# Late images' first quartic by moved tiles, and a rearranged end, in a matrix-root and spectral-convolution kernel

## The chip, the cores and the metric

The kernel runs on one core of a Trainium2 chip. A core has a matrix engine (PE, with its weight loads PEld), a vector engine (DVE), a scalar engine (ACT), GpSimd (POOL) and a sync engine (SP) that only issues DMAs; ACT's queue can issue DMAs too. Each engine works off its own queue in order. The metric is device microseconds of one execution, taken as the median of the runs.

## The reference, cut to what matters

Input x has 32 images of 32 channels, each a 128x128 matrix in 32-bit floats. Two layers follow each other:

```python
def _L0_conv_ref(A):            # matrix square root by Newton-Schulz, 5 steps
    Y = A2 / normA[:, None, None]; Z = I
    for _ in range(5):
        T = 0.5 * (3.0 * I - Z @ Y)
        Y = Y @ T
        Z = T @ Z
    return Y * sqrt(normA)

x = x + _L0_conv_ref(_gn(x))            # _gn: group norm, 16 groups of 2 channels
x = x + _L1_conv_ref(_gn(x), weights1, weights2)
# _L1: 2-d Fourier transform of each channel, the lowest 32 columns and
# 32 + 32 rows of it mixed over channels by weights that differ per mode,
# inverse transform, real part
```

The result is x after both layers.

## The kernel before, in words

**Newton groups.** The root is computed on groups of four channels, 8 groups per image and 256 in all. A group is a generator, `newton`; a `yield` ends a call. The five Newton steps are folded into two quartic polynomials and a last quadratic, so a group makes ten sets of four 128x128 products. Every product needs one operand transposed, and there are two ways to get it. *Near* groups (image 0 and images 19 to 31; `FIRST` is 19) transpose on PE: in `near_quartic` the vector `v` is transposed there, once in each quartic, and `newton` transposes `m` once between them. *Far* groups (images 1 to 18) transpose blocks of 32x32 on DVE (`turned`) and let DMAs put the blocks in place: `across` moves from tile to tile in four DMAs, `away` and `back` go through device memory. The far quartic works with `by_rows`, a view of the moved tile.

**Order.** The order on each engine is the order in which Python issues the instructions. The loop at the end of the kernel works in rounds: it visits nine lanes, calls each lane's group once, and gives steps to side queues in between: `norms` (staging: scaled copies `m` and `mb` of a group, on POOL and ACT), `preps` (statistics of images two ahead, from `xs` tiles), `posts` (`settle`: the store to `mid`, the folds, the statistics of the second layer; then `forward`), `specs` (`spectrum`), `prods` (products with the weights) and `backs` (`inverse`). A far group is started every 26/9 rounds, a near one every 25/5, with at most `LESS` (5) near groups under way. `stage` and `fetch` run ahead: when a group starts, the next is staged and the inputs `b` and `xt` of the third next are fetched.

**The convolution.** It is done in sets of images: `GROUPS` is 20, 7, 3, 2. When a set's last spectrum is there, its products follow (`wide_products` for 20, `small_products` for 7 and 3, `last_products` for the last two), through the tensors `xs`, `od` and `or` in device memory, and then an `inverse` per image: `place` reorders the products into `ob`, PE makes `gt` (tab,ob) and then, in two halves e, four banks `py` (gt,tab), each with a cosine part of 65 columns and a sine part of 63. ACT copies the sine part to `d`, DVE adds the cosine part to both halves of `y` (loaded from `mid`), and `unfold` subtracts and adds `d` on POOL (or DVE for half of them in the tail). `store` writes `y` out, by SP, or by ACT's queue in the tail, when no lane works any more.

**Room.** Tiles come from reserves per name (`rooms`: so many of a pool that lasts, and so many of a pool `early` that is closed when 158 groups are settled). `weights` fetches the weights for `last_products` into tiles that the last groups no longer need.

Of the kernel before, what the change touches and what calls it, by code (L numbers as in the profile page):

```python
# [36 lines left out]
P = 128  # L37
# [56 lines left out]
def conv_preact_kernel(  # L94
# [51 lines left out]

    stp = ctx.enter_context(tc.tile_pool(name="stp", bufs=4))
    up = ctx.enter_context(tc.tile_pool(name="up", bufs=1))
# [73 lines left out]
    def prep(bs, made):  # L222
# [7 lines left out]

        ahead = 3 if first_b else 8

# [74 lines left out]

    rooms = dict(b=(4, 6), xt=(10, 5), x=(3, 2), r=(4, 0), v=(3, 2), w=(3, 2), q=(4, 2))
    rooms.update(my=(4, 3), mb=(2, 4), t=(3, 2), y4=(2, 2), turn=(0, 4))
    turns = dict.fromkeys(rooms, 0)  # L310
# [46 lines left out]
    def is_far(b):  # L357
        return 0 < b < FIRST
# [7 lines left out]
    def fetch(b, g):  # L366
        queue = nc.sync if is_far(b) else nc.scalar
        xt, t = four("xt", has_more(b, g)), four("b", has_more(b, g))
        kept(queue.dma_start(out=t, in_=x[b, :, 4 * g : 4 * g + 4, :]))
        kept(queue.dma_start(out=xt, in_=xt_in[b, :, 4 * g : 4 * g + 4, :]))  # L370
        raw[b, g] = xt, t
# [3 lines left out]
    def staged(b, g, nm, sc, off, sn):  # L375
# [10 lines left out]
        for j in range(4):  # L386
            c = 4 * g + j
            if j < 2 or not is_far(b):
                kept(
# [17 lines left out]
    def near_quartic(m, mb, more):  # L407


        v = plus(m, -QA * MS, products(mb, m), "v", more)  # L410
        yield
        r = four("r", more)
        nc.gpsimd.tensor_tensor(r, mb, eye, ALU.add)
# [24 lines left out]

    def by_rows(t):
        return blocks(t).rearrange("p a c j -> p c a j")  # L440

    def across(t, more):
# [10 lines left out]
        return w  # L453

    def far_quartic(m, mb, v, f, later, more):

        ps = products(m, mb)
        if later:
            held = away(turned(ps, more))
        else:  # L460
            w = across(turned(ps, more), more)
        if later:
            yield
        nc.vector.scalar_tensor_tensor(v, ps, 1 / (9 * MS), v, ALU.mult, ALU.add)
# [13 lines left out]

    def newton(g, sn, xt, m, mb, v, far, more):


        qf, et, eye_t = (QS, EYE_Q, eye_q) if far else (QF, EYE, eye)
        if far:
            q = yield from far_quartic(m, mb, v, 1.0, False, more)
        else:
            q = yield from near_quartic(m, mb, more)
# [24 lines left out]
        else:  # L511
# [3 lines left out]
            yield from rest  # L515
            q = yield from near_quartic(m, mb, more)
            both = [bank().rearrange("p (j k) x -> p j k x", k=2) for _ in range(2)]
            for j in range(4):
# [224 lines left out]
    def small_products(i):  # L743
# [38 lines left out]
        for k2 in range(len(xks)):  # L782
            load_spectra(k2)
        done = None
        for kk in range(KK):
# [36 lines left out]
    def last_products(i):  # L822


        for e in range(2):
            load_input(B - GROUPS[i], e)
        for kk in range(KK):
            if kk % 4 == 0:
                yield
                om = page(f"om{i}_{kk}").rearrange("p (f s o) -> p s f o", f=4, s=8)  # L830
            if kk % 2 == 0:
# [21 lines left out]
            if kk % 4 == 3:  # L853
                for f in range(4):
# [6 lines left out]
                    )  # L861
        warm(9)
        yield

    def weights():


        kinds = [("b", 2)] * 3 + [("x", 2), ("b", 4), ("x", 4), ("x", 10)]
        kinds += [("my", 11)] * 2 + [("r", 12)] * 3 + [("mb", 15)] * 2 + [("v", 15)] * 2
        kinds += [("w", 16)] * 2 + [("my", 16), ("r", 17), ("v", 18)] + [("q", 19)] * 3  # L870
        first = B * C // 4 - 10
# [66 lines left out]
    holding = []  # L938

    def unfold():  # L940

        while sums:
            b, o, y, d = sums.pop(0)
            engine = nc.vector if tail and o % 16 else nc.gpsimd
            for half, op in enumerate((ALU.subtract, ALU.add)):
                yh = y[:, :, 64 * half : 64 * half + 64]
                engine.tensor_tensor(yh, yh, d, op)
            stores.append((b, o, y))

# [20 lines left out]
    def inverse(b):  # L970
# [161 lines left out]
    while todo or any(lanes) or posts or specs or prods or backs:  # L1132
# [3 lines left out]
        for i in range(LANES):  # L1136
# [3 lines left out]
            under_way = [is_far(lane[0]) for lane in lanes if lane]  # L1140
            room = far or under_way.count(False) + 0.6 * under_way.count(True) < LESS
            if lanes[i] is None and todo and room and rounds >= due:
# [4 lines left out]
                xt = ready[0][0]  # L1147
                lanes[i] = (b, g, xt, newton(g, made[b][3], *ready.pop(0), far, has_more(b, g)))
                if stages:
# [91 lines left out]
```

## Time and profile before

| | |
|---|---|
| median of 3 runs | 2969.88 us (2962.28 to 2977.81) |
| the profiled execution's own time | 2972.83 us |
| its span, first to last instruction | 2971.0 us |
| PE, PEld busy | 96%, 90% |
| DVE, ACT, POOL busy | 76%, 52%, 67% |
| DMA | 674.22 MB, mean 227 GB/s |
| PE ident,v (transpositions of v) | 896 instructions, mean 277 ns |
| PE w,v and others (products) | 279 ns mean, two instructions per 128x128 product |
| first group of image 19 starts | about 1498 us |
| last group starts | about 2851 us |
| first instruction of the last set's products | 2917 us |

The tile names in the profile are the program's (`ps<-ident,v` is a PE instruction that writes a bank `ps` and reads `ident` and `v`). All instructions pass through one helper, so their line is always L88, and names tell them apart. `SPq` and `ACTq` are DMA issues. The mean of a PE instruction is from its start to its modelled end, and neighbours overlap; the distance of starts is what it holds the engine for.

### The profile page before, as it was taken

Reading aid. Unit: us, or ns where it says so; the run is one execution under the profiler, and the core shown is the slowest. Engines: PE = TensorE matmul, PEld = TensorE weight load, DVE = VectorE, ACT = ScalarE, POOL = GpSimd, SP = SyncE. Lnnn points to the kernel's source line nnn. Section 1 sums busy time; section 2 is a strip of 40 time slices with the busy share of each in tenths; the row PEclk is TensorE's granted clock in tenths of the full one; section 3 lists DMA queues with packets and bytes.
Section 4 is the critical chain, followed back from the end, with each engine's and each line's share of the span. In section 5 each row is a group of like instructions: output and inputs, shape, how many; then the busy total and the mean of one; then the engine's idle time right before and its main releaser. Section 6 shows DMA issues by size and latency. Waiting matters only on the chain.

```text
span 2971.0 us, 74313 instructions
## 1 busy us (share of the span) xinstructions
PE 2847.8 (96%) x27688; PEld 2666.9 (90%) x27688; DVE 2270.9 (76%) x4407; ACT 1544.7 (52%) x3899; POOL 1986.9 (67%) x2308
## 2 busy tenths in 40 slices
PE   7999999999999999999999999999999999999995
PEld 7899999998999999999999889888888999888983
DVE  7779788888788888888886645886787766777565
ACT  3555555555555555555544445555555544655552
POOL 4677777776767777777665534877778764678453
PEclk9999999999999999999999999999999999999997
DMA  5687878787787878787843566767767747766577
GB/s 174 185 250 244 242 242 251 240 257 231 233 252 217 275 228 263 236 253 239 270 145 98 164 209 210 269 217 271 269 228 268 273 127 222 218 223 225 180 221 260
DMA packets 553078, 674.22 MB, mean 227 GB/s; under 512 B 99344, under 2 KB 333840, under 8 KB 552720
## 3 DMA queue, kind: packets, MB, share of 16 engines
q1 hardware_dynamic: 480576, 536.53, 56.9%
q10 hardware_dynamic: 72144, 132.94, 14.3%
q8 instruction: 222, 3.64, 0.5%
q14 instruction: 136, 1.11, 0.1%
HBM read 402.42 MB, written 229.11 MB: 213 GB/s over the span
## 4 chain that ended last, share of the span: by engine, by line
PE 66%; POOL 11%; DMA 9%; issue 7%; DVE 5%; ACT 1%; SPq 1%; ACTq 0%; DVEq 0%; POOLq 0%
PE ps L88 66%; POOL yt L88 3%; POOL r L88 3%; POOL x L88 2%; DMA w<-turn 2%; POOL fold L88 2%; DMA yt<-mid 1%; DMA b<-in_x 1%; DMA xt<-in_xt 1%; SPq L88 1%; DVE turn L88 1%; DMA xs<-in_xs 1%; DVE yt L88 1%; DMA mid<-xt 1%; DMA out<-yt 1%
## 5 line engine op out<-in xcount | busy, mean ns | idle before, releaser
L88 ACT ACTIVATE my<-ps 128x512 f32<-128x512 f32 x512 | 305.3, 600 | 563.6 <-PE ps L88 443.7
L88 POOL TENSOR_TENSOR fold<-xt 128x256 f32<-128x256 f32 x512 | 363.5, 732 | 285.9 <-DVE xt L88 257.2
L88 ACT ACTIVATE b<-b,a_off,a_sc 128x128 f32<-128x128 f32 x1024 | 469.8, 493 | 97.1 <-issue 15.9
L88 PE MATMUL ps<-my,q 128*128 128x128 f32 (+1 forms) x2944 | 474.4, 309 | 5.7 <-ACT my L88 3.8
L88 PEld LDWEIGHTS ps<-my,q 128*128 128x128 f32 x2944 | 412.9, 192 | 33.0 <-ACT my L88 4.6
L88 POOL TENSOR_TENSOR v<-eye_v,b 128x512 f32<-128x512 f32 x144 | 183.6, 1275 | 382.9 <-ACT b L88 344.6
L88 POOL TENSOR_TENSOR yt<-yt,d 128x512 f32<-128x512 f32 x244 | 306.8, 1281 | 187.4 <-ACT d L88 155.3
L88 PE MATMUL ps<-w,v 128*128 128x128 f32 x2944 | 399.9, 279 | 13.0 <-DVE w L88 10.6
L88 PEld LDWEIGHTS ps<-w,v 128*128 128x128 f32 x2944 | 363.5, 194 | 22.3 <-issue 7.6
L88 DVE STREAM_TRANSPOSE turn<-ps 128x512 f32<-128x512 f32 x432 | 299.7, 702 | 62.2 <-PE ps L88 57.1
L88 ACT ACTIVATE t<-ps 128x256 f32<-128x256 f32 (+1 forms) x368 | 171.0, 467 | 333.3 <-PE ps L88 316.7
L88 POOL TENSOR_SCALAR x<-xt,a_nm,a_sc 128x128 f32<-128x128 f32 x736 | 321.2, 450 | 15.8 <-DVE a_sc L88 15.5
L88 ACT ACTIVATE y<-ps,a_t_s 128x128 f32<-128x128 f32 x1024 | 291.4, 371 | 45.2 <-PE ps L88 45.1
L88 PE MATMUL ps<-q,t 128*128 128x128 f32 x2048 | 273.8, 277 | 0.8 <-DVE v L88 0.8
L88 DVE SCALAR_TENSOR_TENSOR w<-ps,r 128x512 f32<-128x512 f32 x224 | 153.1, 684 | 139.3 <-POOL r L88 71.2
L88 PEld LDWEIGHTS ps<-q,t 128*128 128x128 f32 x2048 | 249.6, 192 | 3.3 <-issue 1.2
L88 DVE BATCH_NORM_STATS2 a_st<-xs 128x6 f32<-128x256 f32 x504 | 185.9, 410 | 64.9 <-DMA xs<-in_xs 64.6
L88 DVE SCALAR_TENSOR_TENSOR q<-ps,eye 128x512 f32<-128x512 f32 x224 | 153.3, 684 | 97.6 <-PE ps L88 94.8
L88 DVE TENSOR_TENSOR xt<-ps,xt 128x512 f32<-128x512 f32 x256 | 174.7, 683 | 40.7 <-PE ps L88 35.2
L88 POOL TENSOR_TENSOR r<-mb,eye 128x512 f32<-128x512 f32 x112 | 142.9, 1276 | 91.8 <-ACT mb L88 91.8
L88 DVE TENSOR_TENSOR yt<-ps,yt 128x512 f32<-128x512 f32 x256 | 163.3, 681 | 39.9 <-PE ps L88 34.4
L88 POOL TENSOR_TENSOR my<-eye_q,my 128x512 f32<-128x512 f32 x144 | 183.8, 1277 | 7.5 <-PE ps L88 7.5
(147 smaller groups left out, 6284.9 us busy)
## 6 DMA issues: line engine op xcount, KB each, us to landing
turn<-turn SPq DMA_DIRECT2D x288, 256.0 KB
mid<-xt SPq DMA_DIRECT2D x256, 256.0 KB
yt<-mid SPq DMA_DIRECT2D x128, 512.0 KB
xs<-in_xs ACTq DMA_DIRECT2D x252, 256.0 KB
out<-yt SPq DMA_DIRECT2D x115, 512.0 KB
b<-in_x SPq DMA_DIRECT2D x144, 256.0 KB
xt<-in_xt SPq DMA_DIRECT2D x144, 256.0 KB
w<-turn SPq DMA_DIRECT2D x576, 64.0 KB
```

Source lines behind the costliest of these rows:

```text
L88: return self.tc.keep_in_program_order(issue(*args, **kw))
```

## The change

1. Groups of images 19 to 31 use a new `late_quartic` as their first quartic: DVE's block transposition and `across` in place of the PE transposition of `v`. The second quartic stays `near_quartic`, in which `r` is now issued a call earlier. These groups' fetches go by SP, and half of the staging of `m` goes from POOL to ACT, as for far groups. Up to six near groups may be under way when no far one is.
2. The reserves are divided anew, and `xs` tiles are six instead of four, loaded five ahead instead of three.
3. Output stores wait until two rounds after their `unfold`, and are looked for in each round.
4. In the last group's calls from the 22nd on, and while products are pending in the tail, no inverse step is issued. `last_products` uses `fold` tiles for the first three of its outputs, and nine warming products at its end go; six are issued in the tail where an inverse loads.
5. For images 30 and 31, the upper and the lower half of an output row are summed in the bank `py` by PE, with a table and its negative, and DVE adds the bank to `y` once: no `d`, no `unfold`.

```diff
-    stp = ctx.enter_context(tc.tile_pool(name="stp", bufs=4))
+    stp = ctx.enter_context(tc.tile_pool(name="stp", bufs=6))
...
-        ahead = 3 if first_b else 8
+        ahead = 5 if first_b else 8
...
-    rooms = dict(b=(4, 6), xt=(10, 5), x=(3, 2), r=(4, 0), v=(3, 2), w=(3, 2), q=(4, 2))
-    rooms.update(my=(4, 3), mb=(2, 4), t=(3, 2), y4=(2, 2), turn=(0, 4))
+    rooms = dict(b=(5, 5), xt=(10, 4), x=(3, 2), r=(3, 0), v=(3, 2), w=(3, 2), q=(3, 3))
+    rooms.update(my=(3, 4), mb=(2, 4), t=(2, 3), y4=(2, 2), turn=(2, 2))
...
-        queue = nc.sync if is_far(b) else nc.scalar
+        queue = nc.sync if b else nc.scalar
...
-            if j < 2 or not is_far(b):
+            if j < 2 or not b:
...
     def near_quartic(m, mb, more):
-        v = plus(m, -QA * MS, products(mb, m), "v", more)
-        yield
         r = four("r", more)
         nc.gpsimd.tensor_tensor(r, mb, eye, ALU.add)
+        v = plus(m, -QA * MS, products(mb, m), "v", more)
+        yield
         yield
         w = plus(transposed(v), 1.0, r, "w", more)
...
+    def late_quartic(m, mb, more):
+        v = minus(eye_v, m, four("v", more))
+        ps = products(mb, m)
+        t = turned(ps, more)
+        yield
+        nc.vector.scalar_tensor_tensor(v, ps, 1 / (9 * MS), v, ALU.mult, ALU.add)
+        w = across(t, more)
+        yield
+        minus(eye_q, mb, mb)
+        yield from rest
+        yield from rest
+        q = plus(products(v, by_rows(w)), 9 / (39 * MS**2), mb, "q", more)
+        yield from rest
+        return q
...
-    def newton(g, sn, xt, m, mb, v, far, more):
-        qf, et, eye_t = (QS, EYE_Q, eye_q) if far else (QF, EYE, eye)
+    def newton(g, sn, xt, m, mb, v, far, late, more):
+        qf, et, eye_t = (QS, EYE_Q, eye_q) if far or late else (QF, EYE, eye)
         if far:
             q = yield from far_quartic(m, mb, v, 1.0, False, more)
+        elif late:
+            q = yield from late_quartic(m, mb, more)
         else:
             q = yield from near_quartic(m, mb, more)
...
@@ small_products, after its first loads
+        yield from rest
...
     def last_products(i):
-        for e in range(2):
-            load_input(B - GROUPS[i], e)
+        load_input(B - GROUPS[i], 0)
+        negative.append(four("y4", False).rearrange("p c x -> p (c x)"))
+        nc.scalar.mul(negative[0][:, 0:256], tab[:, T_IW], -1.0)
...
-                om = page(f"om{i}_{kk}").rearrange("p (f s o) -> p s f o", f=4, s=8)
+                if kk < KK - 4:
+                    om = sets.tile([P, 1024], F32, tag="fold", name=f"om{i}_{kk}", bufs=3)
+                else:
+                    om = page(f"om{i}_{kk}")
+                om = om.rearrange("p (f s o) -> p s f o", f=4, s=8)
...
-        warm(9)
...
     def store():
-        while stores:
-            b, o, y = stores.pop(0)
+        while stores and (tail or rounds - stores[0][3] >= 2):
+            b, o, y, _ = stores.pop(0)
...
             load_input(b, 0)
+            if tail:
+                warm(6)
...
         load_input(b, 1)
+        if negative and more:
+            load_input(b + 1, 0)
+            load_input(b + 1, 1)
         unfold()
         yield
+        if where[b][0] == len(GROUPS) - 1:
+            for e in range(2):
+                py = [bank().rearrange("p c (s h) -> p c s h", s=2) for _ in range(4)]
+                minus_t, plus_t = negative[0][:, 0:256], tab[:, T_IW]
+                parts = [(minus_t, P, 0, 65, 63), (plus_t, P, 1, 65, 63)]
+                parts += [(minus_t, 0, 0, 64, 1), (plus_t, 0, 1, 64, 1)]
+                quads = [slice(32 * i, 32 * i + 32) for i in range(4)]
+                for i, rows in enumerate(quads):
+                    both = gts[e][rows, :, None, 0:64].to_broadcast([32, 4, 2, 64])
+                    nc.tensor.matmul(py[i], plus_t[rows, 0:P], both, start=True, stop=False)
+                for t, at, s, h, n in parts:
+                    for i, rows in enumerate(quads):
+                        nc.tensor.matmul(
+                            py[i][:, :, s, h % 64 : h % 64 + n],
+                            t[rows, at : at + P],
+                            gts[e][rows, :, h : h + n],
+                            start=False,
+                            stop=(h == 64 and s == 1),
+                        )
+                for i in range(4):
+                    y = yts[b, e][i // 2][:, 4 * (i % 2) : 4 * (i % 2) + 4, :]
+                    whole = py[i].rearrange("p c s h -> p c (s h)")
+                    nc.vector.tensor_tensor(y, whole, y, ALU.add)
+                    if i % 2:
+                        o = 16 * e + 4 * (i - 1)
+                        kept(nc.sync.dma_start(out=out[b, :, o : o + 8, :], in_=yts[b, e][i // 2]))
+                if not e:
+                    yield
+            yield
+            return
...
-            room = far or under_way.count(False) + 0.6 * under_way.count(True) < LESS
+            less = LESS if any(under_way) else LESS + 1
+            room = far or under_way.count(False) + 0.6 * under_way.count(True) < less
...
+            if i == 0:
+                store()
...
-            if i == 0 and (turn or holding) or tail and not (posts or specs):
+            at_end = len(steps_of_last) >= 22
+            if i == 0 and (turn or holding) and not at_end or tail and not (posts or specs or prods):
                 step(backs)
```

`weights` takes its tiles some two calls of the last group later than before, since that group has two calls more.

More of the change, by code (lines that the diff above doesn't have):

```diff
@@ L407, in near_quartic @@
     def near_quartic(m, mb, more):
+        r = four("r", more)
+        nc.gpsimd.tensor_tensor(r, mb, eye, ALU.add)
         v = plus(m, -QA * MS, products(mb, m), "v", more)
         yield
-        r = four("r", more)
-        nc.gpsimd.tensor_tensor(r, mb, eye, ALU.add)
         yield
@@ L437, in back @@
         return t
-    def by_rows(t):
-        return blocks(t).rearrange("p a c j -> p c a j")
     def across(t, more):
@@ L453, in across, with by_rows @@
         return w
+    def by_rows(t):
+        return blocks(t).rearrange("p a c j -> p c a j")
+    def late_quartic(m, mb, more):
[12 more added lines that the diff above has]
+        return q
     def far_quartic(m, mb, v, f, later, more):
@@ L459, in far_quartic @@
             held = away(turned(ps, more))
+            yield
         else:
             w = across(turned(ps, more), more)
-        if later:
-            yield
         nc.vector.scalar_tensor_tensor(v, ps, 1 / (9 * MS), v, ALU.mult, ALU.add)
@@ L516, in newton @@
             q = yield from near_quartic(m, mb, more)
+            qf, et, eye_t = QF, EYE, eye
             both = [bank().rearrange("p (j k) x -> p j k x", k=2) for _ in range(2)]
@@ L861, in last_products @@
                     )
-        warm(9)
         yield
     def weights():
-        kinds = [("b", 2)] * 3 + [("x", 2), ("b", 4), ("x", 4), ("x", 10)]
-        kinds += [("my", 11)] * 2 + [("r", 12)] * 3 + [("mb", 15)] * 2 + [("v", 15)] * 2
-        kinds += [("w", 16)] * 2 + [("my", 16), ("r", 17), ("v", 18)] + [("q", 19)] * 3
+        kinds = [("b", 3)] * 3 + [("x", 3), ("b", 6), ("x", 6), ("b", 10), ("x", 12)]
+        kinds += [("my", 13)] + [("r", 14)] * 2 + [("mb", 17)] * 2 + [("v", 17)] * 2
+        kinds += [("w", 18)] * 2 + [("my", 18), ("r", 19), ("v", 20), ("y4", 21)] + [("q", 21)] * 2 + [("q", 23)]
         first = B * C // 4 - 10
@@ L938, in conv_preact_kernel @@
     holding = []
+    negative = []
     def unfold():
@@ L947, in unfold @@
                 engine.tensor_tensor(yh, yh, d, op)
-            stores.append((b, o, y))
+            stores.append((b, o, y, rounds))
     placed = {}
@@ L1147, in conv_preact_kernel @@
                 xt = ready[0][0]
-                lanes[i] = (b, g, xt, newton(g, made[b][3], *ready.pop(0), far, has_more(b, g)))
+                lanes[i] = (b, g, xt, newton(g, made[b][3], *ready.pop(0), far, b >= FIRST, has_more(b, g)))
                 if stages:
```

## The prediction

> **What bounds the kernel now.** I read the page's busy row and slices first, then busy time by 100 us windows, then who waited for whom, then the timeline of a few microseconds, then the chain at the end.
>
> ```profile
> PE 2847.8 (96%) x27688; PEld 2666.9 (90%) x27688; DVE 2270.9 (76%) x4407; ACT 1544.7 (52%) x3899; POOL 1986.9 (67%) x2308
> PEclk9999999999999999999999999999999999999997
> ```
> ```profile
> 400.00:500.00 100.00, 100.00 (x923) 97.00 (x922) 84.68 (x162) 57.08 (x149) 73.70 (x83) 1.00 0.77 232
> 1900.00:2000.00 100.00, 95.73 (x842) 85.78 (x841) 78.07 (x143) 51.38 (x137) 73.53 (x84) 1.00 0.69 235
> 2200.00:2300.00 100.00, 98.24 (x882) 88.91 (x880) 73.23 (x142) 53.16 (x141) 79.59 (x93) 1.00 0.73 254
> 2900.00:2971.00 71.00, 42.16 (x478) 28.64 (x478) 38.67 (x65) 19.26 (x45) 21.55 (x18) 0.74 0.73 254
> ```
>
> The columns are length, PE, PEld, DVE, ACT, POOL, granted clock, DMA share, GB/s. TensorE is over 95% busy at full clock up to 2900 us, in the far stage (row 400) as in the late one (rows 1900, 2200). Only the last 71 us have room. A busy PE could still be a PE whose ends are modelled, so the waits of PE in the stretch with most POOL work (1850 to 2400) come next, with SP's from 1900 to 2400:
>
> ```profile
> PE ps L88 <- DVE q L88: 3.9, 3, 2.1
> PE ps L88 <- DVE w L88: 3.7, 3, 1.9
> PE ps L88 <- ACT my L88: 3.5, 1, 3.5
> ```
> ```profile
> SPq L88 <- POOL yt L88: 150.7, 43, 5.0
> SPq L88 <- DVE yt L88: 80.1, 30, 7.7
> ```
>
> All PE waits there sum to 20.6 us of 550: PE is the bound, though SP, an in-order queue, is held by output stores in pieces of up to 7.7 us.
>
> **The first quartic of 104 late groups (images 19 to 31, 8 groups each).** The cost of a transposition is read from starts, not from the mean duration (277 ns each, which overlap):
>
> ```profile
> 2208.78 0.66 PE L88 MATMUL ps<-ident,v 128*128 128x128 f32 x4
> 2209.27 1.06 PE L88 MATMUL ps<-x,b 128*128 128x128 f32 x8
> 2210.16 1.06 PE L88 MATMUL ps<-q,t 128*128 128x128 f32 x8
> ```
>
> Four transpositions hold PE for 0.49 us (2208.78 to 2209.27; at 2200.90 it is 0.44), eight product instructions for 0.89. One set of four goes per group: 104 x 0.47 = 49 us off the engine that bounds. No product is added: both quartics keep theirs.
>
> The Trainium skill ("TensorE: Matmul & The Clock Gate", Part 4) gives about 275 ns for a PE transpose in a kernel's context and says that such transposes do not engage the full clock. By that rule the sum would be 416 x 0.275 = 114 us, an estimate from that page; the starts above contradict it, and the clock of 0.98 to 1.00 in the late windows does too. The starts decide.
>
> What comes in their place, per group, against a period of 13.1 us (first and last r<-b,eye start at 1497.7 and 2851.4, 103 periods):
> - DVE: out go two scalar_tensor_tensor (v and w, 0.684 each), in come one stream transpose (0.702) and one scalar_tensor_tensor: nothing.
> - POOL: out go one r (1.275) and two of four x staging operations (0.450 each), in come eye_v minus m and eye_q minus mb (1.276 each): +0.38 us. It is hidden while POOL has idle time: 20 to 27% of each window from 1900 to 2400, 2.6 us per period at the tightest.
> - ACT: two more staging operations of 0.49: +1.0 us, on an engine 51 to 58% busy.
> - SP: four tile moves, and two fetches that ACT's queue issued. The far stage's issues take 0.6 us with their waits, so +3.6 us per period; In the wide products SP is fullest: 149 issues of some 0.5 us in 1700 to 1850, half its time; 3.6 of 13.1 us more leaves it under 80%. The fetches pass two DMAs from ACT's queue to SP's, behind mid and out stores; they are issued three starts (39 us) ahead, which covers any SP wait seen (13.3 us at most).
> - DMA: 256 KB more per group at a share of 0.69 to 0.79, against 0.72 to 0.85 in the far stage, which carries three such turns per group.
>
> **The new wait.** PE now waits for w, which is moved. By the yields: turn is written in call 1 of a group's lane, moved in call 2, read by the products in call 7. Five rounds of 13.1 / 5 = 2.6 us are 13 us; four issues take 2.5 of them. Behind the wait stands all of PE's queue. Late groups showed no such move, so I bound it by the far stage. From below: there PE waited 13.4 us in 9 waits for w<-turn among 242 trips (two in each of 121 groups, 300 to 1500), so 104 trips cost 6 us. From above: every trip late by the mean of these nine (1.5 us) is 156 us. When a far trip stood in the chain of waits it took 3.2 to 7.5 us; that fits into the 10 us left, so I take the low end.
>
> The Trainium skill ("DMA: Bandwidth & Descriptors", Anatomy of one DMA) has a fixed cost of about 2 us per DMA (given there for GpSimd's path), which speaks against such moves in small parts. By it the four, overlapping, would need 2.5 + 2 = 4.5 us, an estimate; the chain shows up to 7.5. Either way the wait would be under 10.
>
> Also new: DVE's v waits for POOL's eye_v minus m of one round before, with DVE's q, w and t queued behind it. Before, w waited so for r (47.8 us of DVE idle, 1900 to 2400, of which PE felt 3.7). Now r is issued two rounds ahead of its w. These offset; I take +2 us, between -6 and +10. Reserves (b, xt, r, q, my, t moved between pools): r falls from 4 tiles to 3, but far starts are 2.89 rounds apart and r lives 5 rounds, so it returns 3 rounds early; xt falls from 15 to 14 with some 5 rounds over. Nothing, covered by these rounds. Deeper xs loads can give at most the 64.6 us that DVE waited for them, on an engine that PE outlasts: nothing.
>
> Stage: -49 + 6 + 2 = -41, between -55 (no new wait, -6 for r) and +31 (every second trip late by 1.5 us: 78 in place of 6).
>
> **The end.** Two lines of reading: the DVE stall and the chain.
>
> ```profile
> 2897.09 2.51 DVE L88 TENSOR_TENSOR yt<-ps,yt 128x512 f32<-128x512 f32 x4 [5.23 <-DMA yt<-mid]
> 2899.52 0.68 DVE L88 SCALAR_TENSOR_TENSOR t<-ps,eye 128x512 f32<-128x512 f32 x1
> 2904.84 0.69 DVE L88 TENSOR_TENSOR xt<-ps,xt 128x512 f32<-128x512 f32 x1 [4.64 <-PE ps L88]
> ```
> ```profile
> 2934.04 6.17 DMA or<-od
> 2940.29 1.06 ACT ob L88
> 2941.40 2.13 PE ps L88 x16
> ...
> 2964.85 1.67 DVEq L1235
> ```
>
> - The last Newton group's t waits behind an inverse step's yt (5.23 + 2.4 us) and its last product behind PE's 2.08 us for tab,ob. No inverse step is issued in its last four rounds any more. Between 0 (the stall moves a round earlier) and 9: I take 4. It has two rounds more (26 calls instead of 24): cost 0 to 5, take 2.
> - The last products run without the image's steps between: gt,tab (1.57) and the page wait that set om's last copy at 2929.92, against 2917 + 8.2 + 0.7 = 2925.9 for the products alone: 4 us, between 0 and 6. Image 29's two steps (some 5 us of DVE) move under od's 9.7 us (2930.55 to 2940.29); if that cover is short, they cost up to 5.
> - Images 30 and 31: 30.7 us from ob to the end. PE's work per half image doubles in columns (1024 for 512 per row group): sixteen instructions took 1.15 us at full clock, 1.9 at the low one, so 2.3 to 3.8. DVE keeps four additions (0.68 each, 2.7), and the d copies and unfolding go. Start 1.1 + 2.1 + 0.6, four times 2.7 to 3.8, 2.1 for image 31's first product and 4.5 for the last store: 21 to 26. Take 24: -7. With the added 0.4 us of table and six warming products instead of nine, both beside waits for od, nothing else.
>
> End: -4 + 2 - 4 - 7 = -13, between -25 and +5.
>
> **Sum.** -41 - 13 = -54. The profiled execution took 2972.83 (span 2971.0), so it would be 2919; the median of the runs is 2.95 below it, so 2916.
>
> **The rivals.**
> 1. *POOL paces the stretch.* The chain from 1844 to 2144 runs through POOL (yt, r, x, fold). For it: 80% busy plus waits for ACT d. Against: PE's waits there. If it decides, the 43 groups of 1850 to 2400 save no 20 us and add 43 x 0.38 = 16: 2916 + 36 = 2952.
> 2. *The moved tiles arrive late (slower).* SP is held by out stores and the wide products' weights, and w arrives after its five rounds. It decides from 54 / 104 = 0.5 us of PE wait per late group. For it: SP's waits above, and a DMA share that rises by some 8 points. Against: the far stage has less time to spare per round of queue and pays 0.06 us per trip; stores are now held until their unfolding is two rounds old. At 1.5 us for every second group, +78 - 6: 2988.
> 3. *The saving is eaten* by the in-order engines behind PE (ACT +1.0, POOL +0.38 per group), and only the end gains: 2970 - 13 = 2957.
>
> **How the numbers follow.** Forecast 0.70 (own range 2895 to 2940), rival 1 0.12, rival 3 0.09, rival 2 0.09. Changes under 0.5% (15 us, and the three runs spread over 15.5) can't be told from none. Rival 1 (0.6% faster) is split 0.09 faster, 0.03 same; rival 3 is same; rival 2 is slower. With 0.02 of the forecast's upper tail in same: faster 0.77, same 0.14, slower 0.09. The range goes from the lowest corner of the bounds (2970 - 55 - 25 = 2890, less 4 for the runs' spread) to just over rival 3, and leaves out rival 2 and the tails: 2886 to 2958.
>
> **What would show it.** Right: ident,v down from 896 to 480 instructions; the late period down from 13.1 to about 12.7 us; PE over 95% busy there; PE waits for w<-turn under 15 us in the late stage; POOL at 83 to 88% from 1900 to 2400; from the last xt to the end some 50 us instead of 66. Wrong: PE waits for w<-turn of tens of us (rival 2), POOL near 95% with PE waiting for DVE v (rival 1), the far stage's length changed by the tile reserves, or a first inverse step after the last products that lasts longer than od's trip.

## The result, and the profile after

The changed kernel takes 2979.77 us (median of 20 runs, 2971.68 to 2990.9) against 2967.89 for the kernel before: a ratio of 1.0044, 95% interval 1.0033 to 1.0055. That is 0.4% slower. It lies inside the 0.5% that the prediction counted as no difference, but the interval excludes 1, and the forecast of 2916 and its whole range of 2886 to 2958 were wrong. The profiled execution took 2987.89 us, its span 2986.1.

Below, "group" counts the groups of four channels from 0 in the order in which they run; 152 is the first of image 19. A stage runs from the issue of one group's store to `mid` to that of another. A ratio is always to the kernel before on the same chip, with its 95% interval; a difference between two kernels is taken from their two ratios, so it is good to some 0.2 to 0.3%, 6 to 9 us (0.1% is 3 us). Stages come from one profile of each kernel, and which product and inverse steps fall into a stage can differ between kernels.

The page after, its busy row and the clock in 40 slices:

```profile
PE 2826.0 (95%) x27362; PEld 2640.5 (88%) x27362; DVE 2288.0 (77%) x4403; ACT 1608.0 (54%) x4092; POOL 2011.9 (67%) x2192
PEclk9999999999999999999999999999999999999997
```

PE does 21.8 us less work in a span that is 15.1 us longer. The work that the change names is gone: the group of the transpositions has 480 instructions in place of 896, as forecast.

```profile
L88 PE MATMUL ps<-ident,v 128*128 128x128 f32 x480 | 73.0, 275 | 1.3 <-DVE v L88 1.3
```

The windows of 100 us after (length, PE, PEld, DVE, ACT, POOL, granted clock, DMA share, GB/s), at the same places as before:

```profile
400.00:500.00 100.00, 99.92 (x919) 96.74 (x911) 84.81 (x162) 57.75 (x150) 75.16 (x84) 1.00 0.78 237
1900.00:2000.00 100.00, 95.44 (x837) 85.68 (x836) 83.27 (x151) 58.06 (x155) 79.23 (x80) 1.00 0.86 277
2200.00:2300.00 100.00, 93.35 (x826) 84.12 (x826) 77.36 (x134) 55.02 (x145) 77.58 (x78) 0.98 0.84 274
2900.00:2986.00 86.00, 58.14 (x687) 41.80 (x685) 45.78 (x82) 25.89 (x56) 21.23 (x19) 0.80 0.86 293
```

The far stage (row 400) is as it was, and its end moved by 0.3 us (group 144's store at 1504.2 us before, 1503.9 after): the new reserves cost nothing. Over the profiles of all runs that store lies between 1495 and 1518 us, with the old division and with the new. In row 2200 PE fell from 98 to 93% busy. PE was given less to do and uses it to wait. The waits of PE from 1850 to 2400 us say for whom (total, times, longest); the first fence is the `fold` row before, the second is after:

```profile
PE ps L88 <- POOL fold L88: 1.8, 3, 0.8
```
```profile
PE ps L88 <- POOL fold L88: 14.1, 8, 2.7
PE ps L88 <- DVE q L88: 6.0, 6, 1.6
PE ps L88 <- DVE xt L88: 3.5, 3, 1.5
```

All waits there make 40.5 us where they made 20.6: POOL's `fold` now comes late. But this stretch does not hold most of the loss: groups 176 to 224 took 641.6 us instead of 637.5, and groups 224 to 240 even 195.2 instead of 210.2, with 1684 PE instructions in that stage instead of 1906. The next fences are one stage each, from group 160's store to group 176's, of the kernel before and of the changed one:

```profile
1651.00:1875.00 224.00, 217.98 (x2556) 197.82 (x2555) 126.47 (x255) 108.37 (x262) 103.98 (x139) 1.00 0.64 203
```
```profile
1649.00:1900.00 251.00, 229.24 (x2576) 205.19 (x2575) 133.50 (x267) 124.96 (x314) 121.10 (x134) 0.97 0.67 207
```

This is the stage of the wide products (set of 20 images). The same 16 groups take 27 us longer, PE idles 21.8 us instead of 6.0, and the granted clock falls from 1.00 to 0.97. PE's waits there, before and after:

```profile
PE ps L88 <- DMA plain<-xs: 4.9, 3, 2.4
PE ps L88 <- DMA diag<-in_wk: 0.5, 1, 0.5
```
```profile
PE ps L88 <- DMA plain<-xs: 10.6, 5, 3.6
PE ps L88 <- DMA diag<-in_wk: 3.5, 1, 3.5
```

PE waits 14.1 us, not 5.4, for the loads of the wide products, which is 8.7 of the 15.8 us by which its idle time grew; the rest is in smaller waits, the largest 2.7 us for POOL's `fold`. It does not wait for the moved tile: from 1500 to 2880 us PE's waits for `w<-turn` are 0.3 us in all. SP's queue shows how the two hang together (timeline after: start, duration, engine, what):

```profile
1725.79 2.49 SPq L88 DMA_DIRECT2D w<-turn  x4
1728.38 1.43 SPq L88 DMA_DIRECT2D od<-om  x1
1729.90 2.12 SPq L88 DMA_DIRECT2D diag<-in_wk  x4
1732.07 0.42 SPq L88 DMA_DIRECT2D plain<-xs  x1
1732.59 1.77 SPq L88 DMA_DIRECT2D diag<-in_wk  x4
1735.80 1.73 PE L88 MATMUL ps<-diag,plain 128*32 128x128 f32 x32 [3.55 <-DMA diag<-in_wk]
```

SP issues in order. The four moves hold it 2.49 us, an `od` store that waits for its copy 1.43 us, and only then come the weights, for which PE stands 3.55 us. From the first of the weights' 128 loads (`diag<-in_wk`) to the last, SP's DMA issues held it for 78 us of 139 before (56%, 167 issues) and for 111 of 148 after (75%, 218 issues).

### The profile page after: what moved, and what is told of

Read it like the earlier page. It is cut to its first block, busy times and chain, and to the rows that moved or that the text cites. A ratio compares the mean times of both kernels' runs of the same rounds, so it can differ in the third digit from the quotient of the medians.

```text
span 2986.1 us, 74514 instructions
## 1 busy us (share of the span) xinstructions
PE 2826.0 (95%) x27362; PEld 2640.5 (88%) x27362; DVE 2288.0 (77%) x4403; ACT 1608.0 (54%) x4092; POOL 2011.9 (67%) x2192
## 5 line engine op out<-in xcount | busy, mean ns | idle before, releaser
L88 ACT ACTIVATE b<-b,a_off,a_sc 128x128 f32<-128x128 f32 x1024 | 492.0, 500 | 39.9 <-DMA xs<-in_xs 16.6
L88 DVE STREAM_TRANSPOSE turn<-ps 128x512 f32<-128x512 f32 x536 | 374.1, 705 | 165.1 <-PE ps L88 154.7
L88 POOL TENSOR_TENSOR yt<-yt,d 128x512 f32<-128x512 f32 x232 | 291.6, 1278 | 162.4 <-ACT d L88 160.0
L88 ACT ACTIVATE x<-xt,a_off,a_sc 128x128 f32<-128x128 f32 x496 | 250.6, 505 | 15.1 <-DMA xs<-in_xs 7.6
L88 POOL TENSOR_SCALAR x<-xt,a_nm,a_sc 128x128 f32<-128x128 f32 x528 | 232.3, 451 | 16.2 <-DVE a_sc L88 14.9
L88 DVE BATCH_NORM_STATS2 b_st<-xt 128x6 f32<-128x256 f32 x512 | 186.5, 404 | 0.0
```

What stands on the lines that cost most here:

```text
L88: return self.tc.keep_in_program_order(issue(*args, **kw))
```

## The experiments

The first theory was that the late quartic costs time because of what it puts on the queues behind PE (SP, POOL, ACT); its rivals were that the end or the held stores cost it, or that the far stage's reserves do.

**late_off: all of the change but the late quartic itself.**

```diff
-newton(..., far, b >= FIRST, has_more(b, g))
+newton(..., far, False, has_more(b, g))
```

> The changed kernel with the late quartic alone undone: groups of images 19 to 31 transpose v on PE again (near quartic first), while fetches on SP, staging on ACT, reserves, held stores and the new end stay. SP theory (the moved tiles and the fetches fill SP's queue and the wide products' loads come late) and POOL theory (POOL, with 0.38 us more per group, paces the late stage): the moves bring about what they cost, so without them the time is 2965 to 2980, and the stretch 1650 to 1900 gets shorter by 10 to 25 us. End-and-stores theory (the moves save their 49 us and something else in the change loses 60): 3020 to 3035.

Measured: 2958.67 us beside 2968.08, 0.9970 [0.9947, 0.9993]. That is below the 2965 to 2980 expected. So the late quartic costs 0.74%, 22 us, and the rest of the change gains 9. The stage of the wide products is whole again:

```profile
1663.00:1880.00 217.00, 216.97 (x2550) 197.00 (x2550) 128.18 (x253) 119.33 (x294) 91.88 (x108) 1.00 0.65 214
```

**late_only: parts 1 and 2 alone.** Held stores and the whole end are taken back; the core of it:

```diff
-        while stores and (tail or rounds - stores[0][3] >= 2):
+        while stores:
...
-        if where[b][0] == len(GROUPS) - 1:
+        if negative:
```

> The kernel before with the first two parts only (late quartic with its fetches, staging and six lanes; reserves and six xs tiles); stores, the end and the last two images as before. SP and POOL theories: the loss is made by these parts, 2975 to 2990. End-and-stores theory: 2920 to 2940.

Measured: 2993.98 us beside 2968.08, 1.0091 [1.0069, 1.0114]: +27 us. The loss comes from these two parts, and the rest takes back some 14.

**fetch_act: the late fetches back on ACT's queue.**

```diff
-        queue = nc.sync if b else nc.scalar
+        queue = nc.sync if is_far(b) else nc.scalar
```

> The changed kernel with the fetches of images 19 to 31 back on ACT's queue. SP theory: SP has 0.8 to 1 us less per group and the wide products' weights no longer wait behind fetches; 2955 to 2970, PE waits for diag and plain in 1650 to 1900 fall from 14 us to under 5. POOL theory: 2976 to 2984, no change.

Measured: 3005.71 us, 1.0128 [1.0105, 1.0151]: 25 us slower than the change, not faster. PE's waits for ACT's `mb` from 1500 to 2880 us rose from 5.1 to 11.9 us, and those for the wide loads stayed (13.0 for `plain<-xs`). So it isn't the mere number of SP's issues. That a late group's extra copies on ACT come late behind ACT's own two fetches is the likely reading, but these waits are 7 of the 25 us. The Trainium skill ("DMA: Bandwidth & Descriptors", Issuing engines are not separate DMA queues) says that issuing on several engines saves only the sequencer's time, usually small beside the DMA. Here the choice of the issuing engine was worth 25 us, twice what the whole change cost. What stands in order behind the issue is the likely reason; no run shows it alone.

**late_from_28: the late quartic for images 28 to 31 only** (`b >= 28`).

> The changed kernel with the late quartic for images 28 to 31 alone (32 groups), where neither the wide products nor the wide set's inverse steps run. Both theories (the loss is made where SP is full, groups 160 to 176, and where POOL is, 176 to 224): 2947 to 2956, below late_off's 2959 by 32 x 0.47 = 15 us at the most. If the late quartic costs the same anywhere: 2959 + 21 x 32 / 104 = 2965.

Measured: 2969.74 us beside 2965.35, 1.0011 [0.9991, 1.0031]: 12 us more than late_off, for 32 groups that lie after the wide products, more than the terms found below would give them. In its profile groups 200 to 224, ahead of the edit, took 321.6 us (late_off 315.2), and groups 224 to 240 took 216.8 (204.6), though late_off's profiled execution, 2970.92 us, lies 12 us above that kernel's median. I have no cause for that; it stays open.

**no_unfold: without the arithmetic of `unfold` for images 0 to 19.** It tests whether POOL, which the waits for `fold` point at, holds PE.

```diff
+                if GROUPS[where[b][0]] > NB:
+                    continue
```

> The changed kernel without the subtraction and addition that unfold makes on POOL for images 0 to 19 (left out, so the upper and lower halves of these output rows lack the sine part); POOL loses 160 of its 1.28 us operations and all its waits for ACT's d between 1850 and 2450. POOL theory: the PE idle time of that stretch (34 us of 500) falls to under 12 and the kernel takes 2950 to 2962. SP theory: 2972 to 2980.

Measured: 2942.03 us beside 2968.08, 0.9921 [0.9901, 0.9942]: 37 us less than the change, below the 2950 to 2962 expected. The stage of groups 176 to 224 took 607.2 us instead of 641.6.

**before_no_unfold: the same on the kernel before.** The control, without which no_unfold would be read wrongly.

> Control: the kernel before without unfold's subtraction and addition for images 0 to 19 (left out as in no_unfold). If PE bound the kernel before and POOL only the changed one: 2960 to 2968, under 8 us gained. If POOL held the kernel before as much: 2930 to 2945.

Measured: 2940.52 us beside 2965.35, 0.9920 [0.9897, 0.9944]: 24 us less. So two thirds of what no_unfold showed was there before the change. PE, 96% busy with 20 us of waits in 550, was not the only bound of the kernel before. How much of the 24 us is POOL's time and how much the earlier release of the output stores isn't separated.

**unfold_later: is it the amount of POOL's work, or its order?** The same work, but an `unfold` is issued at least two rounds after its sums, with stores held one round instead of two.

```diff
-        while stores and (tail or rounds - stores[0][3] >= 2):
+        while stores and (tail or rounds - stores[0][3] >= 1):
...
-        while sums:
-            b, o, y, d = sums.pop(0)
+        while sums and (tail or rounds - sums[0][4] >= 2):
+            b, o, y, d, _ = sums.pop(0)
...
             if i == 0:
+                unfold()
                 store()
```

> The changed kernel with each unfold issued two rounds later, so that POOL does not stand in its queue for ACT's d while r, x, v and fold wait behind. POOL theory, as a matter of order: POOL's waits for d (98 us in 1900 to 2540) mostly go, groups 176 to 224 get 10 to 30 us shorter, 2950 to 2970. If POOL's work and not its order is the bound: 2976 to 2984.

Measured: 2949.54 us beside 2965.35, 0.9942 [0.9922, 0.9962]: 30 us less than the change, and faster than both kernels. POOL's waits from 1900 to 2400 us, of the kernel before, the changed one, and this one:

```profile
POOL yt L88 <- ACT d L88: 86.0, 26, 7.6
POOL fold L88 <- DVE xt L88: 15.5, 12, 4.3
```
```profile
POOL yt L88 <- ACT d L88: 78.0, 26, 5.5
POOL fold L88 <- DVE xt L88: 1.2, 2, 0.6
```
```profile
POOL yt L88 <- ACT d L88: 26.9, 21, 2.9
POOL fold L88 <- DVE xt L88: 17.0, 13, 3.0
```

The idle fifth of POOL was not all free room: 78 to 86 us of the 500 was the engine standing in its queue for ACT's `d`, with a group's `x`, `r` and `fold` behind it. The second row tells how far behind it is: before, `fold` still waited for its input (15.5 us), so POOL was on time; after, it hardly does (1.2), and PE waits for `fold` instead.

**before_unfold_later and off_unfold_later: the same order on the kernel before, and with the late quartic off.** The second is unfold_later with late_off's edit.

> The kernel before with each unfold two rounds later and each output store one round after it, and nothing else of the change. As before_no_unfold gained 25 us by leaving the unfolding out, of which some is order and some is work: 2942 to 2958. If order doesn't matter here: 2962 to 2970.

> late_off with each unfold issued two rounds later: a version without the late quartic. If POOL's order matters without the late quartic too: 2925 to 2945, below unfold_later's 2950. If it matters only because of the late quartic's POOL work: 2954 to 2962.

Measured: 2952.61 us beside 2966.66, 0.9952 [0.9935, 0.9969]; and 2941.67 beside 2966.66, 0.9921 [0.9899, 0.9942]. The second is 15 us below late_off, and also below unfold_later by 6 (within what these runs can tell): even with POOL's stalls eased, the late quartic gains nothing. The first is 14 us below the kernel before; but it also delays the stores, and held_stores below, which delays the stores alone, gives 13 (0.9957). On the kernel before, the order of the unfolding thus shows no gain of its own. The 30 and 15 us were measured on kernels whose stores were held already; there the stores leave a round later too, so even these two are not the order's alone.

**off_pool: what does +0.38 us of POOL per late group cost?** late_off with one more POOL operation, unread, in each late group.

```diff
+        if extra:
+            minus(eye_v, m, four("turn", more))
```

> late_off with one more POOL operation (1.28 us, eye_v minus m into a tile that nothing reads) in the first quartic of each late group: the change's extra POOL work by itself, 133 us on an engine with 20% of idle time. POOL theory: 10 to 30 us longer than late_off, 2969 to 2989, most of it in groups 176 to 224. If POOL has room, as predicted: under 4 us, 2955 to 2963.

Measured: 2975.0 us beside 2966.66, 1.0031 [1.0011, 1.0050]: 18 us above late_off. The operation takes 1.285 us, 104 times: 134 us of POOL's time. Most of it did fit into POOL's idle time; 18 us reach the end. late_off stages on ACT what the kernel before staged on POOL, as the change does; so this operation stands for the ones that the late quartic itself adds.

**off_moves: the four moves alone, with nobody waiting for them.** late_off with `across(v, more, "turn")` in each late group.

> late_off (PE transposition in the late groups) plus four tile moves per late group on SP, of the same size and at the same call as the change's, from v into a tile that nothing reads: the moves' cost by itself, without their gain and without the extra POOL work. SP theory (the moves in SP's queue delay the wide products' loads): groups 160 to 176 take 235 to 250 us as in the changed kernel (late_off: 217.5) and the kernel 2975 to 2995. POOL theory alone: within 6 us of late_off's 2959, and that stretch stays under 225.

Measured: 2968.81 us beside 2965.35, 1.0013 [0.9999, 1.0028]: 13 us above late_off, for DMAs whose data nobody reads; less than the 2975 to 2995 us, and the 235 to 250 us of the stage, that were expected if the moves alone made the loss. The stage of the wide products shows the same 13 (231 us against late_off's 217):

```profile
1651.00:1882.00 231.00, 223.81 (x2588) 202.52 (x2587) 132.73 (x264) 121.11 (x302) 93.20 (x110) 0.99 0.70 221
```

**no_moves: the change without its moves.**

```diff
-        w = across(t, more)
+        w = t
```

> The changed kernel without the four moves: the second product of the late quartic reads the block-transposed tile itself (so the late images' roots are wrong), everything else as in the change, its saving, its POOL work and its two more calls. If the parts add up (saving -26, POOL +16 on late_off's 2959): 2945 to 2955, and the moves with the wait for them make the other 25 to 30 us of the changed kernel's 2980. If the structure (two more calls, DVE's v behind POOL's v, the bank held over a round) makes the remainder: 2962 to 2975.

Measured: 2951.11 us beside 2969.45, 0.9937 [0.9918, 0.9955]. The change is 1.07% above it: moves with a reader cost 32 us. PE's waits for the wide loads fall to

```profile
PE ps L88 <- DMA plain<-xs: 2.1, 2, 1.4
PE ps L88 <- DMA diag<-in_wk: 0.3, 1, 0.3
```

and the stage takes 231 us instead of 251:

```profile
1650.00:1881.00 231.00, 219.97 (x2533) 198.17 (x2531) 128.77 (x258) 122.44 (x308) 116.33 (x129) 0.99 0.65 205
```

That is still 13 us more than late_off's 217, though no move is left and PE has less to do. So of the 33 us by which this stage grew against late_off, 20 went with the moves. What makes the other 13 was not found: PE idles 11 us there, the largest waits being for POOL's `r` (2.8) and ACT's `mb` (2.1), and off_pool's stage stayed at 218. From group 160 to group 224 the two kernels are 5 us apart. Without moves the late quartic gains 10 us on late_off, not the 49 of its PE time.

**later_from_23: unfold_later with the late quartic only for images 23 to 31** (`b >= 23`), so that no move meets the wide products.

> unfold_later with the late quartic for images 23 to 31 alone, so that no group transposes by moves while the wide products load their weights through SP. If the stretch of the wide products is where the moves cost: groups 160 to 176 take 216 to 222 us instead of 242 and the kernel 2922 to 2935, below off_unfold_later's 2942. If the late quartic costs everywhere: 2942 to 2950.

Measured: 2945.45 us beside 2969.45, 0.9912 [0.9888, 0.9936]. The stage of the wide products takes 219.5 us (unfold_later 242.4), so the loss there is avoided, yet the whole is no better than off_unfold_later: for 72 groups outside that stage the late quartic is worth nothing that can be measured. By stages, it takes 13 us more than off_unfold_later in groups 176 to 224 and 12 less in groups 224 to 240.

**off_no_turn, unfold_no_turn and one_of_four: what is a transposition worth?** late_off without the four PE transpositions of each late group, the same on off_unfold_later, and late_off with one of four kept.

```diff
-        w = plus(transposed(v), 1.0, r, "w", more)
+        w = plus(v if bare else transposed(v), 0.0 if bare else 1.0, r, "w", more)
```
```diff
+            ps = bank()
+            nc.tensor.transpose(ps[:, 0, :], v[:, 0, :], ident)
+            ps = ps[:, 0:1, :].to_broadcast([P, 4, P])
```

> late_off with PE's transposition of v left out in the first quartic of images 19 to 31 (w is made from r alone, so these images' roots are wrong): the prediction's saving of 104 x 0.47 = 49 us by itself, with no move, no wait and no POOL work in its place. If PE is the bound of the late stage, as predicted: 2905 to 2918. If the in-order queues of POOL and DVE hold the stage about as much as PE: 2930 to 2955 (late_off 2959).

> off_unfold_later with PE's first transposition of v left out in images 19 to 31 (as in off_no_turn, these images' roots are wrong): the saving by itself where POOL no longer stands waiting for ACT's d. If POOL's order ate the missing half of the saving (26 of 49 on late_off): 2892 to 2905, 37 to 50 below off_unfold_later's 2942. If the other half is lost in PE's and DVE's own short waits whatever POOL does: 2910 to 2922.

> late_off with one PE transposition of v in place of four in the late groups' first quartic (its result stands for all four channels, so these images' roots are wrong); w reads the bank as before, where off_no_turn's w read two operands in SBUF and took 0.92 us instead of 0.68. Three quarters of 49 us go from PE: 37. If off_no_turn's 26 was short because its w was slower: 2920 to 2930, 29 to 37 below late_off's 2959. If the other engines hold back half of the saving anyway: 2936 to 2946.

Measured: 2932.87 us beside 2966.66, 0.9886 [0.9863, 0.9910], 25 us below late_off; 2912.36 beside 2967.78, 0.9812 [0.9793, 0.9832], 32 below off_unfold_later by the ratios and 29 by the medians; and 2935.04 beside 2968.82, 0.9885 [0.9864, 0.9906], 25 below late_off. The first two share a flaw: reading `v` from the same memory as `r` made each `w` slower (916 ns on average in off_no_turn, 871 in unfold_no_turn). The group of `w` in off_no_turn and in late_off (busy us, mean ns):

```profile
L88 DVE SCALAR_TENSOR_TENSOR w<-v,r 128x512 f32<-128x512 f32 x104 | 95.2, 916 | 0.7 <-POOL r L88 0.6
```
```profile
L88 DVE SCALAR_TENSOR_TENSOR w<-ps,r 128x512 f32<-128x512 f32 x224 | 152.8, 683 | 76.3 <-PE ps L88 65.5 <-POOL x L88 8.1 <-POOL r L88 1.3
```

one_of_four is free of that: `w` still reads the bank at 683 ns, and three of four transpositions, 104 x 0.47 x 3/4 = 37 us of PE's time, are gone. It gives 25: two thirds of PE's time comes through. Scaled to four, the saving is 33 us, an estimate. unfold_no_turn has POOL's stalls eased and gives 32 with the slower `w`, 7 more than off_no_turn, which is within what these runs can tell. So whether POOL's order holds back the last third can't be said; what does has not been found.

**held_stores: part 3 alone, on the kernel before.**

```diff
-        while stores:
-            b, o, y = stores.pop(0)
+        while stores and (tail or rounds - stores[0][3] >= 2):
+            b, o, y, _ = stores.pop(0)
...
+            if i == 0:
+                store()
```

> The kernel before with the third part alone: output stores held until two rounds after their unfold. late_only was 14 us slower than the changed kernel and the end alone made nothing, so if the stores matter by themselves (SP no longer stands at a store whose unfold is not done): 2950 to 2960. If they matter only beside the moved tiles: 2964 to 2972.

Measured: 2953.58 us beside 2967.78, 0.9957 [0.9941, 0.9972]: -13 us, from the part that the prediction gave no term. SP's wait for the unfolding, from 1900 to 2400 us, is not what went; it was 150.7 us before:

```profile
SPq L88 <- POOL yt L88: 154.8, 59, 4.8
```

So what the held stores gain is shown, and why is not.

**end_only: parts 4 and 5 alone, on the kernel before**, with the pause of inverse steps from the 20th call (this group has two calls fewer).

> The kernel before with the end alone: no inverse step in the last group's last four rounds, fold tiles for om, the last two images summed on PE, warming moved; stores are not held. By the prediction's term for the end: 13 us less (2953), between -25 and +5. If late_only's difference to the changed kernel (14 us) came from the held stores instead: 2962 to 2970.

Measured: 2972.32 us beside 2969.45, 1.0000 [0.9983, 1.0016]. The end is worth nothing. In its profile groups 240 to 255 took 178.3 us against 186.3 before, and from the last store to `mid` to the end it is 73.5 us against 62.0: what the last groups gain, the tail takes back.

## Why the prediction was wrong, point by point

**-49 us, the transpositions.** The count and the hold per group were right, and so was the reading that the engine is held for 0.47 us and not for four means of 277 ns. What failed is "off the engine that bounds": of 37 us taken off PE, 25 reached the end. The term measures about -33.

**+6 us, the new wait.** This is the step that failed most: the term measures +32, 26 us above the forecast (below its upper bound of 156). The wait itself is even smaller than forecast, 0.3 us. I priced the moves by who waits for the moved tile. I had SP's share in the wide products (half, rising to "under 80%"; it measured 56% and 75%), and took that as covered. But a queue that issues in order and waits at its head delays whoever is behind long before it is full, and behind were the products' weights. off_moves shows it with data that nobody reads: +13. The other 19 come with moves that have a reader and wait for their source; the profile of SP after, 1900 to 2400 us, has such waits (below), but that they account for all 19 was not tried. In the wide products PE's gaps cost more than themselves: the profile's clock shows 17.1 us at half speed in that stage after, and none before.

**POOL, "+0.38 us, hidden".** Not wholly hidden: a single further operation of 1.28 us per group, unread, cost 18 us of its 134. (The 0.90 us of staging that went to ACT, the other part of the +0.38, is in late_off, which shows no gain beyond that of its held stores.) What stood behind POOL's idle time was not asked. The chain of waits had shown it (the prediction's rival 1 names "waits for ACT d"), and the argument against, few waits of PE, was the mistake: 20.6 us of waits stood there, and taking the unfolding away still gave 24. The first reading was also a little high: PE was not over 95% busy all the way to 2900 us, but 93 to 94% in the windows from 800 and 2000 and 91% from 2800.

**The stage.** Against late_off: -33 (transpositions) + 18 (POOL) + 32 (moves) = +17, where the change measured +22, within the runs' 6 to 9 us. The first two make -15, where no_moves measured -10. Rival 2 was right about the place ("wide products' weights") and the engine, SP, and wrong about what is late. later_from_23 does not contradict these terms: for 72 of 104 groups outside the wide products, (-33 + 18) x 72/104 is -10 if the 13 us of the moves all belong to that stage, and (-33 + 18 + 13) x 72/104 is -1 if they don't; -3 was measured, good to 6 to 9. So rival 1 and rival 3 were each half right: by these terms POOL, and perhaps SP, eat most of the saving outside the wide products, and inside them SP's moves make most of the loss.

**Reserves, 0.** Right: the far stage ends at the same time.

**Held stores, no term.** -13 us, all that late_off gains (9) and more. The prediction named them only as an argument against rival 2. The hazard that it read, SP's waits of 150.7 us for POOL's `yt`, is as large with held stores alone (154.8). It is smaller after, but the moves do that, not the held stores: late_off has 132.7 us, off_moves 47.4, and late_only, without held stores, 34.0. After, with the next row:

```profile
SPq L88 <- POOL yt L88: 50.6, 22, 4.3
SPq L88 <- DVE w L88: 39.7, 11, 7.1
```

The second row is new (1.1 us before): SP now stands 39.7 us for DVE's `w` at the head of its queue, and 23.6 us for `turn`, the source of the moves. The prediction's longest wait of SP, 13.3 us, was not the longest: one of 15.8 stands at 2606 us before, still well under the 39 us by which fetches run ahead.

**The end, -13.** It measured 0. From the last `xt` to the end it took 70.9 us, not some 50, and 66.2 before. The last `xt` and then the chain of waits, after:

```profile
2915.24 0.69 DVE L88 TENSOR_TENSOR xt<-ps,xt 128x512 f32<-128x512 f32 x1 [1.31 <-PE ps L88]
```
```profile
2938.04 2.11 DMA od<-om
...
2940.43 5.69 DMA out<-yt
...
2946.59 6.42 DMA yt<-mid
...
2953.02 2.41 DVE yt L88 x4
...
2959.30 1.06 ACT ob L88
...
2960.41 2.13 PE ps L88 x16
```

The sums in PSUM gave 4 of the 7 us: 26.8 us from `ob` to the end instead of 30.7. The DVE stall of 5 us ahead of the last `t` went too. From `xt` to the first of the last products it is 12.5 us, as before (12.2). What failed is the step that put image 29's steps under `od`'s trip at "up to 5". From the first product (2927.76) to `ob` it takes 31.5 us instead of 23.3. SP shows why:

```profile
2930.60 8.00 SPq L88 DMA_DIRECT2D od<-om  x8
2938.64 8.65 SPq L88 DMA_DIRECT2D yt<-mid  x4
2947.52 8.46 SPq L88 DMA_DIRECT2D or<-od  x4
```

The last `od` in the chain lands at 2940.15; `or` is issued from 2947.52, behind the `y` loads of the held steps, which wait in SP's queue for output stores to free their tiles. And `ob` follows when image 29's sums leave DVE. It is the same fault in reading as with the moves: the steps were counted in DVE's time, their loads ahead of `or` on SP not at all.

**What stays open:** the lost third of the transpositions' time, 19 of the moves' 32 us, the 13 us of the wide products' stage that stay without moves, why held stores gain, and late_from_28's 12 us.

The best versions with the whole arithmetic are off_unfold_later (0.9921) and later_from_23 (0.9912), which can't be told apart: both delay `unfold` and hold the stores, and neither has the late quartic in the wide products.

## What to carry to other kernels

Before work is moved from the fullest engine to the idle time of another, ask what that idle time is: where an in-order engine stands for an input at the head of its queue, work put into its idle time can still cost (here 18 us of 134), and its share of busy time does not say so. Price a DMA not by when its own reader needs it but by what is issued after it on its queue, above all loads that feed the bound engine. And test "this engine is the bound" by taking some of its work away: here 37 us of PE's time were worth 25, and issuing one helper's work two rounds later, on kernels that held their stores, was worth 15 to 30.

## What the runs showed of the hardware

- A DVE operation of 128x512 took 916 ns with both operands in SBUF and 683 with one in PSUM, in a stage where POOL works most of the time, and POOL's own `yt` grew from 1284 to 1312 ns. The Trainium skill ("SBUF — State Buffer", Who interferes with whom) has a DVE instruction with two SBUF inputs contend with GpSimd's reads; both numbers agree with that, and so does the trace of off_no_turn one by one: the 47 of its 104 operations that met an idle POOL took 681 ns on average, the 45 that POOL worked beside all the time 1034. With one operand in PSUM, in late_off, it was 684 with POOL idle and 682 with POOL at work.
- Stretches of 3.4 us (or 6.8) at half clock began within 5 us of the start of gaps of PE of 1.4 to 3.6 us (one of 6.0): 48 us of them from group 144's store to group 255's after, 24 us before. Not every such gap had one; that of 2.6 us at 2099 us after had none. The twelve gaps after that did make some 27 us; if half clock halves PE's work, an estimate, the 48 us cost another 24, nearly as much again.
- Four moves of 64 KB per group, which nobody read, cost 13 us over 104 groups (0.12 us per group), beside a DMA share that rose from 0.72 to 0.81 in the windows after the wide products.
